# Inverting the softmax sums on GpSimd, as a power of minus one, in a cross-attention kernel

## The chip, the core and the metric

The kernel runs on one core of a Trainium2 chip. A core has five engines that work at the same time, each through its own queue in order: TensorE (PE in the profile; its weight loads are PEld), VectorE (DVE), ScalarE (ACT), GpSimd (POOL) and SyncE (SP), which here only issues DMAs. They wait for each other by semaphores. SBUF is the memory on the chip with 128 partitions; PSUM, in eight banks, takes what TensorE computes. The metric is the device time of one execution in microseconds. Before the change it is 497.91 us, the median of 2 runs (497.78 to 498.04).

## What is computed

The kernel is a cross-attention layer in float32: 2 batches of 2048 tokens with 640 channels, 20 heads of 32 channels, and a context of 154 rows a batch. The first 77 rows of the context are text, the other 77 have key and value weights of their own; each half has its own softmax, and the two results are added.

```python
text = encoder_hidden_states[:, :TEXT_LEN, :]
ip = encoder_hidden_states[:, TEXT_LEN:, :]
q = _split_heads(hidden_states @ Wq.T, H)
k = _split_heads(text @ Wk.T, H)
v = _split_heads(text @ Wv.T, H)
out_text = _merge_heads(_attend(q, k, v, sm_scale))
k_ip = _split_heads(ip @ Wk_ip.T, H)
v_ip = _split_heads(ip @ Wv_ip.T, H)
out_ip = _merge_heads(_attend(q, k_ip, v_ip, sm_scale))
out = out_text + IP_SCALE * out_ip
out = out @ Wo.T + bo
return out + residual
```

`_attend` takes softmax(q k^T / sqrt(32)) v. So each token has, for each head, two rows of 77 scores; each row has its own maximum, its own sum of exponentials, and its own inverse of that sum.

## The kernel before

The work is cut into pairs and units. A *pair* q (0 to 9) is a batch and a chunk of 128 channels, which is four heads. A *unit* u (0 to 19) is a pair and a half of the tokens, 1024 of them; unit u belongs to pair u // 2. A unit's 1024 tokens are eight tiles of 128, in three *groups* s of 3, 3 and 2 tiles (`GROUPS`). A group has its tokens on the 128 partitions and, in its free dimension, 3 x 4 x 2 x 77 = 1848 scores (12 x 154), or 1232 for the group of two tiles. So there are 20 x 3 = 60 groups, 40 large and 20 small. A large group has 24 sums for each partition, a small one 16.

A group goes through these steps, each a word in a long schedule (letter, group number, unit):

- `R`: TensorE computes the scores into four PSUM banks (`scores`, L233).
- `K`: ScalarE copies them to the buffer `pb` in SBUF (`take`, L245). For a few groups (`DIRECT`) this step is missing and the later ones read PSUM.
- `M`: VectorE finds the maxima (`maxima`, L281 and L284).
- `S`: GpSimd subtracts them (`subtract`, L295). Groups listed in `BIASED` or `DIRECT` have the subtraction in the exponential instead.
- `E`: ScalarE takes exponentials (L301 for a whole group, L269 row by row). For the 13 groups in `SUMMED` the row-by-row form also accumulates the sums, `den`.
- `D`: for the 47 other groups VectorE sums the exponentials (`sums`, L306).
- `I`: the sums are inverted, `rden` from `den` (`invert`, L311), on VectorE.
- `N`: GpSimd multiplies the group by `rden` (`normalise`, L316).
- `T`: VectorE transposes the group in blocks of 32 (`transpose`, L323).

When all six groups of a pair are transposed, `A` has TensorE multiply them with the values (`attend`, L332), and `CA` has ScalarE copy the result out (L355, L359). Between these, TensorE also computes the queries (`q`, L201), the keys and values (`k`, `v`, L142), and, from about 220 us on, the output product of the first batch (`m`, `o`, L471, L490, L500), whose parts VectorE adds up (`cm`, L515 and L521) and for which GpSimd forms differences of tokens (`G`, L431) and of weights (`W`, L401). After the last attention the output product of the second batch follows (L828 and L834 for the sums on VectorE and GpSimd, L848 for the matmuls, L792 and L794 for adding up).

The order is not found while the program runs. `SCHEDULE` is one list of such words, written out by hand; `emit` goes through it and puts each step's instructions into the queue of its engine. Each engine works strictly in that order and waits at an instruction whose inputs are not there. A piece of the list, lines 570 and 571, around three inversions:

```python
"N1.2 E0.3 M1.3 E2.3 k.2.0@4 D0.3 S1.3 q.5.0@5 LK.12 SQ.1 T1.2 VS.1.1 cq.4.1 ck.2.0 E1.3 D2.3 I0.3 R2.4@0 "
"D1.3 cq.5.0 N0.3 R0.4@1 K2.4 LK.13 v.2.0@0 VS.1.0 I2.3 K0.4 M2.4 N2.3 T0.3 E2.4 q.6.0@2 I1.3 T2.3 N1.3 "
```

The tiles `mx`, `den` and `rden` of one size rotate through four buffers each (`small`). The transposed groups lie in three zones of `pb`; a unit's zone is written again by a later unit's `K`. Loads and stores (`LK`, `LQ`, `LX`, `VS`, `SF`, `SS`) are issued by SyncE.

Of the kernel before, what the change touches and what calls it, by code (L numbers as in the profile page):

```python
# [9 lines left out]
F32 = mybir.dt.float32  # L10
AF = mybir.ActivationFunctionType
ALU = mybir.AluOpType
# [8 lines left out]
def kernel(  # L21
# [25 lines left out]
    nc = tc.nc  # L47
    P = 128
# [31 lines left out]
    const = ctx.enter_context(tc.tile_pool(name="const", bufs=1))  # L80
# [17 lines left out]
    pb = const.tile([P, SUB + 1, NT, G, LP], F32, name="pb")  # L98
    nc.gpsimd.memset(pb[:, :, :, :, 2 * L :].rearrange("p z n g l -> p (z n g) l"), 0.0)

    vT = const.tile([P, B, LP], F32, name="vT")
    nc.gpsimd.memset(vT[:, :, 2 * L :], 0.0)
    vS0 = [const.tile([P, LP], F32, name=f"vS0_{n}") for n in range(2)]
# [150 lines left out]
    dens = {}  # L254
# [53 lines left out]
    def invert(u, s):  # L308
        n = GROUPS[s][1] * G
        rden = small.tile([P, n, 2], F32, tag=f"rden{n}", name=f"rden_{u}_{s}")  # L310
        nc.vector.reciprocal(rden, dens[(u, s)])  # L311
        rdens[(u, s)] = rden

    def normalise(u, s):
# [317 lines left out]
    def emit(word):  # L632
# [28 lines left out]
        elif k[0] in "KMSEDINT":  # L661
            ps = at[f"R{i}.{x}"]
            if k[0] == "K":
                take(x, i, ps)
            elif k[0] in "ME":
                direct, biased = (x, i) in DIRECT, (x, i) in BIASED
                if k[0] == "M":
                    maxima(x, i, ps if direct else None, biased)
                elif direct or biased:
                    exponential_of(  # L670
                        x, i, ps if direct else None, den_of(x, i) if (x, i) in SUMMED else None
                    )
                else:
                    exponential(x, i)
            else:
                dict(S=subtract, D=sums, I=invert, N=normalise, T=transpose)[k[0]](x, i)
# [214 lines left out]
```

## Time and profile before

All times in microseconds, from the one profiled execution, whose span is 496.7; the median of the runs without these details is 497.91.

| what | busy | share of the span | instructions |
|---|---|---|---|
| TensorE matmuls | 490.3 | 99% | 4114 |
| VectorE | 408.5 | 82% | 412 |
| GpSimd | 362.5 | 73% | 157 |
| ScalarE | 315.0 | 63% | 1021 |

The costliest groups on VectorE and GpSimd, from the groups of the page:

| step | engine | count | busy | mean of one, ns | idle before it |
|---|---|---|---|---|---|
| normalise (L316) | GpSimd | 60 | 176.1 | 2944 | 39.7 |
| subtract (L295) | GpSimd | 38 | 119.3 | 3152 | 51.8 |
| transpose (L323) | VectorE | 60 | 115.7 | 1932 | 4.9 |
| maxima (L281) | VectorE | 51 | 93.7 | 1850 | 30.7 |
| sums (L306) | VectorE | 47 | 88.7 | 1895 | 17.6 |

Busy means that an instruction of the engine is running; an engine that waits for a semaphore is idle. PE is busy for nearly the whole span, so time before a normalisation or a transpose costs something only where PE in turn waits for it.

### The profile page before, as it was taken

What the parts mean: (1) busy time and instruction counts of PE and PEld (TensorE: products, weight loads), DVE (VectorE), ACT (ScalarE), POOL (GpSimd) and SP (SyncE); (2) the same over time, 40 slices, a digit from 0 to 9 for tenths busy, and PEclk for the clock granted to TensorE, in tenths of its full rate; (3) what the DMA queues carried; (4) which work ended last, traced back from release to release, by engine and by line L of the source; (5) the groups of instructions that cost most, each with busy time, mean ns of one, the idle gap of its engine ahead of it and who ended that gap; (6) DMA issues with size and microseconds to landing.
All of it is one profiled execution on the core that took longest, in us unless ns stands there. A gap on an engine that the chain in (4) does not pass through costs nothing.

```text
span 496.7 us, 10482 instructions
## 1 busy us (share of the span) xinstructions
PE 490.3 (99%) x4114; PEld 287.9 (58%) x4114; DVE 408.5 (82%) x412; ACT 315.0 (63%) x1021; POOL 362.5 (73%) x157
## 2 busy tenths in 40 slices
PE   8999999999999999999999999999999999999997
PEld 5676657657547556456647654755755675444442
DVE  0069989979979989969976896687999978898877
ACT  1165878978978778668999786587578966100000
POOL 0069978798888999989874858565899888284830
PEclk9999999999999999999999999999999999999999
DMA  8991440332360454886445177418525401420115
GB/s 259 356 246 40 132 120 1 106 93 69 92 213 3 132 178 132 274 273 237 158 152 191 58 244 210 133 57 246 174 69 171 127 23 43 149 84 1 43 73 223
DMA packets 67474, 69.38 MB, mean 140 GB/s; under 512 B 5473, under 2 KB 47201, under 8 KB 67425
## 3 DMA queue, kind: packets, MB, share of 16 engines
q1 hardware_dynamic: 66704, 68.00, 43.8%
q8 instruction: 32, 0.52, 0.5%
q10 hardware_dynamic: 720, 0.72, 0.4%
q14 instruction: 18, 0.14, 0.1%
HBM read 54.94 MB, written 10.49 MB: 132 GB/s over the span
## 4 chain that ended last, share of the span: by engine, by line
PE 92%; DMA 3%; SPq 1%; DVE 1%; POOL 1%; ACT 1%; issue 0%; POOLq 0%
PE bank L201 33%; PE bank L848 11%; PE bank L490 10%; PE bank L233 10%; PE bank L332 10%; PE bank L142 9%; PE bank L471 6%; PE bank L500 3%; DMA aT<-in_L_xattn_Wk_ip_dram 2%; DMA wq<-in_L_xattn_Wq_dram 2%; SPq L534 1%; POOL pb L316 1%; DVE den L306 0%; ACT pb L301 0%; SPq L132 0%
## 5 line engine op out<-in xcount | busy, mean ns | idle before, releaser
L316 POOL TENSOR_TENSOR pb<-pb,rden 128x1848 f32<-128x1848 f32 (+1 forms) x60 | 176.1, 2944 | 39.7 <-DVE rden L311 35.5
L201 PE MATMUL bank<-x,wq 128*128 128x512 f32 x400 | 180.4, 601 | 0.6 <-DMA x<-in_x_dram 0.5
L295 POOL TENSOR_TENSOR pb<-pb,mx 128x1848 f32<-128x1848 f32 (+1 forms) x38 | 119.3, 3152 | 51.8 <-DVE mx L281 51.5
L201 PEld LDWEIGHTS bank<-x,wq 128*128 128x128 f32 x400 | 74.1, 191 | 86.7 <-issue 80.8
L323 DVE STREAM_TRANSPOSE pb<-pb 128x1920 f32<-128x1920 f32 (+1 forms) x60 | 115.7, 1932 | 4.9 <-POOL pb L316 4.3
L281 DVE TENSOR_REDUCE mx<-pb 128x24 f32<-128x1848 f32 (+1 forms) x51 | 93.7, 1850 | 30.7 <-ACT pb L245 30.5
L245 ACT COPY pb<-bank 128x462 f32<-128x462 f32 (+1 forms) x204 | 87.2, 539 | 36.0 <-PE bank L233 35.4
L306 DVE TENSOR_REDUCE den<-pb 128x24 f32<-128x1848 f32 (+1 forms) x47 | 88.7, 1895 | 17.6 <-ACT pb L301 13.3
L301 ACT ACTIVATE pb<-pb 128x1848 f32<-128x1848 f32 (+1 forms) x38 | 64.2, 1696 | 17.8 <-POOL pb L295 17.5
L269 ACT ACTIVATE pb<-pb,mx 128x77 f32<-128x77 f32 x224 | 67.8, 364 | 0.3 <-DVE mx L281 0.2
L233 PEld LDWEIGHTS bank<-kT,qT 32*128 32x128 f32 x1280 | 45.4, 184 | 26.9 <-issue 15.6
L269 ACT ACTIVATE pb<-bank,mx 128x77 f32<-128x77 f32 x184 | 51.8, 386 | 9.3 <-DVE mx L284 9.3
L233 PE MATMUL bank<-kT,qT 32*128 32x154 f32 x1280 | 56.2, 305 | 0.3 <-ACT kT L559 0.3
L332 PE MATMUL bank<-pb,v 32*32 32x512 f32 x1600 | 55.2, 597 | 0.0
L142 PE MATMUL bank<-wo_ct,aT 128*128 128x154 f32 x320 | 45.6, 296 | 0.3 <-DMA aT<-in_L_xattn_Wk_ip_dram 0.3
L142 PEld LDWEIGHTS bank<-wo_ct,aT 128*128 128x128 f32 x320 | 42.9, 188 | 3.6 <-issue 2.2
L332 PEld LDWEIGHTS bank<-pb,v 32*32 32x32 f32 x1600 | 29.9, 103 | 22.8 <-issue 10.7
L211 ACT ACTIVATE qT<-bank 128x512 f32<-128x512 f32 x40 | 24.2, 619 | 22.1 <-PE bank L201 22.0
L471 PE MATMUL bank<-aT,wo_ct 128*128 128x512 f32 x80 | 36.1, 596 | 0.0
L269 ACT ACTIVATION_READ_ACCUMULATOR pb<-bank,mx 128x1 f32 x128 | 33.6, 267 | 0.0
L490 PE MATMUL bank<-aT,wo_ct 128*128 128x256 f32 x128 | 32.3, 385 | 0.0
L490 PEld LDWEIGHTS bank<-aT,wo_ct 128*128 128x128 f32 x128 | 23.7, 190 | 6.5 <-issue 3.0
(75 smaller groups left out, 434.4 us busy)
## 6 DMA issues: line engine op xcount, KB each, us to landing
x<-in_x_dram SPq DMA_DIRECT2D x20, 1280.0 KB, 6.7
out_dram<-acc SPq DMA_DIRECT2D x20, 256.0 KB, 2.3
x<-in_x_dram SPq DMA_DIRECT2D x18, 256.0 KB, 5.9
acc<-in_x_dram SPq DMA_DIRECT2D x16, 256.0 KB, 4.7
out_dram<-x SPq DMA_DIRECT2D x15, 256.0 KB, 2.0
v<-vS SPq DMA_DIRECT2D x160, 20.0 KB, 2.8
wq<-in_L_xattn_Wq_dram SPq DMA_DIRECT2D x9, 320.0 KB, 5.0
aT<-in_L_xattn_Wk_dram SPq DMA_DIRECT2D x5, 512.0 KB, 5.5
```

The lines of the kernel that those rows point to most:

```text
L142: nc.tensor.matmul(keys_in(out), loaded[n][:, k, :], cT[:, k, :, t, :], start=(k == 0), stop=(k == NCC - 1))
L201: nc.tensor.matmul(pq, wqs[q % 3][:, k, :], xs[place_of(u, h)][:, k, :], start=(k == 0), stop=(k == NC - 1),)
L233: nc.tensor.matmul(ps[g][:, ts(t, 2 * L)], qTs[(u, h)][g * D : (g + 1) * D, ts(st, P)], kT[g * D : (g + 1) * D, c, b].rearrange("p t l -> ...
L245: nc.scalar.copy(keys_of(u, s)[:, :, g], ps[g][:, : n * 2 * L].rearrange("p (n l) -> p n l", n=n))
L269: nc.scalar.activation(row, row if ps is None else rows_in(ps[g], n)[:, t, x], AF.Exp, bias=maxs[(u, s)][:, *one], accum_out=None if den i ...
L281: nc.vector.tensor_reduce(mx, rows_of(u, s), AX.X, ALU.max, negate=negate)
L295: nc.gpsimd.tensor_tensor(rows_of(u, s), rows_of(u, s), maxs[(u, s)].unsqueeze(3).to_broadcast([P, n, 2, L]), ALU.subtract)
L306: nc.vector.tensor_reduce(den_of(u, s), rows_of(u, s), AX.X, ALU.add)
L316: nc.gpsimd.tensor_tensor(rows_of(u, s), rows_of(u, s), rdens[(u, s)].unsqueeze(3).to_broadcast([P, n, 2, L]), ALU.mult)
L323: nc.vector.transpose(p, p)
L332: nc.tensor.matmul(pa[r][g * D : (g + 1) * D, :], v4s[q % 2][rows, g, k, :], zones[rows, :, g, k, :], start=(k == 0), stop=(k == NK - 1),)
L490: nc.tensor.matmul(part, w_of[m][:, kp, op], t_of(m, b, i)[:, kp], start=(op == kp == 0 and m in (1, 2, 5)), stop=(op == 1 and kp == 1 and ...
```

## The change

The reciprocal of each group's sums on VectorE becomes a two-input operation on GpSimd: the sums to the power of a constant minus one, which stands in a column of its own and is read with a step of zero for all 24 (or 16) sums. The constant is written once by a memset on GpSimd ahead of the loops. The words of the schedule keep their places, so the power enters GpSimd's queue where `I` stands: after the last `S`, `N`, `G` or `W` before it in the list and ahead of the next one, which in 48 of the 60 cases is the normalisation of the same group. The normalisation, which waited for VectorE, then follows its power on the same engine.

```diff
     pb = const.tile([P, SUB + 1, NT, G, LP], F32, name="pb")
     nc.gpsimd.memset(pb[:, :, :, :, 2 * L :].rearrange("p z n g l -> p (z n g) l"), 0.0)
 
+    minus = const.tile([P, 1], F32, name="minus")
+    nc.gpsimd.memset(minus, -1.0)
     vT = const.tile([P, B, LP], F32, name="vT")
...
     def invert(u, s):
         n = GROUPS[s][1] * G
         rden = small.tile([P, n, 2], F32, tag=f"rden{n}", name=f"rden_{u}_{s}")
-        nc.vector.reciprocal(rden, dens[(u, s)])
+        nc.gpsimd.tensor_tensor(rden, dens[(u, s)], minus.unsqueeze(2).to_broadcast([P, n, 2]), ALU.pow)
         rdens[(u, s)] = rden
```

## The prediction

> **What bounds the kernel now.** I read the page first (busy shares, the slices, the chain), then the windows by stretch, the groups by form, the waits of GpSimd (POOL), and last the timeline where TensorE (PE) is nearest to waiting.
>
> ```profile
> span 496.7 us, 10482 instructions
> ...
> PE 490.3 (99%) x4114; PEld 287.9 (58%) x4114; DVE 408.5 (82%) x412; ACT 315.0 (63%) x1021; POOL 362.5 (73%) x157
> ...
> POOL 0069978798888999989874858565899888284830
> ...
> PE 92%; DMA 3%; SPq 1%; DVE 1%; POOL 1%; ACT 1%; issue 0%; POOLq 0%
> ```
>
> PE is busy for 99% of the span and the chain is PE's for 92%. The change takes nothing off PE, so what it can do is to make PE wait. GpSimd, which gets the new work, stands at 8 or 9 tenths over long stretches. The windows cut the part with attention into four, which I chose so that each is either tight or loose for GpSimd. The second fence has the same windows for the reciprocals alone.
>
> ```profile
> core 0: us, PE busy (x) PEld busy (x) DVE busy (x) ACT busy (x) POOL busy (x), PEclk, DMA share, GB/s
> 20.00:70.00 50.00, 49.41 (x371) 31.75 (x382) 39.78 (x29) 30.94 (x67) 38.12 (x13) 1.00 0.58 164
> 70.00:255.00 185.00, 184.83 (x1918) 112.11 (x1917) 169.85 (x135) 152.62 (x430) 160.40 (x59) 1.00 0.44 135
> 255.00:347.00 92.00, 91.76 (x820) 54.28 (x789) 69.76 (x85) 70.91 (x325) 61.94 (x25) 1.00 0.54 171
> 347.00:424.00 77.00, 76.88 (x712) 49.21 (x707) 69.53 (x74) 55.19 (x191) 68.59 (x37) 1.00 0.34 105
> ```
>
> ```profile
> 20.00:70.00 50.00, 1.51 (x6) 1.00 0.58 164
> 70.00:255.00 185.00, 8.15 (x31) 1.00 0.44 135
> 255.00:347.00 92.00, 3.01 (x11) 1.00 0.54 171
> 347.00:424.00 77.00, 3.34 (x12) 1.00 0.34 105
> ```
>
> PE is idle for 0.17 + 0.24 + 0.12 = 0.53 us from 70 to 424 us: a relief can win hardly more than that. POOL is idle for 11.9, 24.6, 30.1 and 8.4 us, with 6, 31, 11 and 12 inversions to take in. How much PE has in hand shows at the attention of the pair that starts at 211.57 us (rows of POOL, DVE and PE):
>
> ```profile
> 191.59 3.29 POOL L295 TENSOR_TENSOR pb<-pb,mx 128x1848 f32<-128x1848 f32 x1 [1.00 <-DVE mx L281]
> 194.83 2.26 POOL L316 TENSOR_TENSOR pb<-pb,rden 128x1232 f32<-128x1232 f32 x1
> 197.04 3.30 POOL L295 TENSOR_TENSOR pb<-pb,mx 128x1848 f32<-128x1848 f32 x1
> 200.28 8.75 POOL L316 TENSOR_TENSOR pb<-pb,rden 128x1232 f32<-128x1232 f32 x3
> ...
> 205.45 5.79 DVE L323 STREAM_TRANSPOSE pb<-pb 128x1280 f32<-128x1280 f32 x3
> ...
> 211.57 1.92 PE L332 MATMUL bank<-pb,v 32*32 32x512 f32 x49
> ```
>
> POOL runs from 191.59 to 209.03 us with no gap, four normalisations in it; the last transpose ends at 205.45 + 5.79 = 211.24 us, and PE takes its result 0.33 us later. POOL's queue is the second bound, a third of a microsecond behind PE.
>
> **The change part by part.** Prices come from these groups (mean ns behind the comma):
>
> ```profile
> L316 POOL TENSOR_TENSOR pb<-pb,rden 128x1848 f32<-128x1848 f32 x40 | 131.3, 3288 | 24.8 <-DVE rden L311 22.7 <-ACT aT L355 1.1 <-ACT pb L245 0.6
> ...
> L316 POOL TENSOR_TENSOR pb<-pb,rden 128x1232 f32<-128x1232 f32 x20 | 45.1, 2255 | 14.9 <-DVE rden L311 12.8 <-ACT kT L686 2.1
> ...
> L311 DVE RECIPROCAL rden<-den 128x24 f32<-128x24 f32 x40 | 11.6, 290 | 5.4 <-ACT pb L269 4.8
> ...
> L834 DVE TENSOR_TENSOR pb<-aT 128x1024 f32<-128x1024 f32 x7 | 8.3, 1221 | 1.7 <-PE bank L332 1.5 <-ACT aT L359 0.2
> ...
> L834 POOL TENSOR_TENSOR pb<-aT 128x1024 f32<-128x1024 f32 x3 | 7.1, 2381 | 2.3 <-PE bank L848 2.3
> ...
> L311 DVE RECIPROCAL rden<-den 128x16 f32<-128x16 f32 x20 | 4.8, 240 | 0.8 <-ACT pb L269 0.7
> ...
> L828 POOL TENSOR_TENSOR pb<-pb,wo_ct 128x128 f32<-128x128 f32 x9 | 4.4, 500 | 10.9 <-DVE pb L828 10.9
> ...
> L401 POOL TENSOR_TENSOR x<-x,wo_ct 128x512 f32<-128x512 f32 x1 | 1.3, 1274 | 0.1
> ```
>
> *Removed:* 60 reciprocals, 11.6 + 4.8 = 16.4 us of VectorE (DVE), and the 6.2 us for which DVE stood still before them, mostly for sums that ScalarE (ACT) accumulates. DVE is not what PE waits for, beyond the 0.53 us above: I count 0. In front of a normalisation that waited, 0.29 us goes.
>
> *Added, the constant:* one memset of a column before the loops, where POOL has no other work: 0.
>
> *Added, 60 powers on POOL.* The trace has no power. Lower end: a plain operation of that size. The two forms of the normalisation give (3288 − 2255)/(1848 − 1232) = 1.68 ns an element and 0.19 us fixed, so 0.23 us for 24 elements and 0.22 for 16; less than an ordinary operation with two inputs is excluded, as this one reads two inputs too. Upper end: as much as a whole normalisation, 3.29 and 2.26 us, the costliest thing POOL does here. Between them I take a logarithm, a product and an exponential as some twenty elementary steps, each at 1.68 ns an element (the twenty is my estimate, the step is the row's): 0.19 + 24 × 0.0336 = 0.99 us and 0.19 + 16 × 0.0336 = 0.73 us, 0.90 us in the mean of 40 and 20. The nearest row in size, the 128x128 operation at 0.50 us, holds for one step an element, so I stay above it. Behind each power its normalisation waits for it on the same engine; the dependent row above (L401) started 0.1 us after its predecessor. So a group costs POOL 1.0 us, 60 us in all.
>
> *What waits behind it.* The power takes the wait for the sums that the normalisation had, so it delays nothing new by waiting: POOL's queue behind is the normalisation, then the next subtraction. In 12 of 60 places another group's instructions lie between a power and its own normalisation, mostly another power; that moves a power ahead by one place, and I add nothing. No DMA and no other queue is touched.
>
> *What of the 60 us is hidden.* POOL's own waits tell, here for 70 to 255 us:
>
> ```profile
> POOL pb L316 <- DVE rden L311: 11.5, 10, 2.5
> POOL pb L295 <- DVE mx L281: 10.9, 8, 3.0
> ```
>
> A wait before a subtraction, for maxima, comes from PE's scores and can take up lateness. A wait before a normalisation cannot, as the power needs the same sums; there the 0.29 us of the reciprocal is gained. So this stretch covers 10.9 + 10 × 0.29 = 13.8 us of 31 × 1.0: 17.2 us show. By the same count the first stretch covers 2.1 us (its other idle time is before the first group) of 6: 3.9 show. From 255 to 347 us, 11.7 + 6 × 0.29 = 13.4 cover 11: 0 show. From 347 to 424 us, 0.8 + 1.7 (two other waits) + 8 × 0.29 = 4.8 cover 12: 7.2 show. These are the rows, in that order:
>
> ```profile
> POOL pb L295 <- DVE mx L281: 30.3, 2, 28.2
> ...
> POOL pb L316 <- DVE rden L311: 20.7, 6, 6.1
> POOL pb L295 <- DVE mx L281: 11.7, 4, 5.5
> ...
> POOL pb L316 <- DVE rden L311: 5.8, 8, 2.1
> POOL x L834 <- PE bank L500: 0.9, 1, 0.9
> POOL pb L828 <- DVE pb L828: 0.8, 1, 0.8
> POOL pb L295 <- DVE mx L281: 0.8, 2, 0.6
> ```
>
> (2.1 is 30.3 less the one wait of 28.2 before the first subtraction.) Sum: 3.9 + 17.2 + 0 + 7.2 = 28.3 us. After 424 us there is no normalisation and the rest only shifts. Span 496.7 + 28.3 = 525.0 us; the median of the two runs, 497.91, lies 1.2 above the span, so the time is 526.2 us. With c for the cost of a group, the slowdown is 49c − 20.7 (49 groups in the three stretches that show), and above c = 1.22 the loose stretch adds 11c − 13.4. Were none of it covered, it would be 60 us; were every idle moment of POOL of use, (31 − 24.6) + (12 − 8.4) = 10 us.
>
> **The rivals.**
>
> *A power is a plain operation (not slower).* 0.23 and 0.22 us, c = 0.33: every stretch covers it (10.2 of 13.8 us in the longest) and the time stays at 498 us. For it: nothing on the page says that this operation is dearer than a product. Against it: reciprocals on DVE take 290 and 240 ns, 6.2 ns an element, where DVE's sum at L834 takes 1221 ns for 1024 elements, 1.2 at most. An inversion is several steps there too. It decides below c = 0.63 (a mean power of 0.53 us), where 49c − 20.7 is under 10 us, 2% of the time.
>
> *A power is the reciprocal at POOL's pace.* The same sum (L834) takes 2381 ns on POOL and 1221 on DVE, 1.95 times. So 0.57 and 0.47 us, c = 0.63, 49 × 0.63 − 20.7 = 10.2 us: 508 us, on the edge of 2%. The Trainium skill (GPSIMD Engine Reference, section 4.1, Engine selection) has that rule: elementwise work with two inputs runs about twice as slow on GpSimd as on VectorE. By that rule the time is this rival's, and the L834 rows agree with it. Against it: DVE's reciprocal is its own instruction, while a general power has an exponent to deal with.
>
> *A power is worked out at length.* As dear as the normalisation it serves, c = 2.94 + 0.1 = 3.04: 49 × 3.04 − 20.7 + 11 × 3.04 − 13.4 = 148 us, 646 us. For it: a power in software with its special cases. Against it: 24 elements would cost what 1848 cost now.
>
> *The relief decides (faster).* DVE's 22.6 us come free and some transposes are earlier. Even with free powers PE has 0.53 us to win after 70 us and 0.59 us before: 496.8 us.
>
> **How the numbers follow.** Likeliest, c of about 0.75 to 1.8 (514 to 572 us): 0.46, forecast 526.2 us. Plain operation: 0.14. POOL's pace: 0.17, half of it within 2%. At length: 0.22. Relief: 0.01. A measurement of this kernel tells about 2% (10 us) from no change: faster 0.01; within 2%, 0.14 + 0.08 = 0.22; slower, 0.46 + 0.09 + 0.22 = 0.77. The range runs from 500 us (c = 0.47, most of the plain case left out below) to 610 us (60c − 34.1 = 112 at c = 2.4, two thirds of the lengthy case left out above); about 0.2 is outside.
>
> **What would show it.** In the profile after: 60 powers on POOL by their line, each 0.7 to 1.0 us; the reciprocal's rows gone and DVE's busy time down by 16; normalisations about 0.1 us behind their powers; PE's idle time in the four windows up by 4, 17, 0 and 7 us, in waits before attention, scores and queries, and the chain going through POOL there; from the last attention to the end, the same length as now. A power under 0.5 us makes the forecast wrong towards 498 us, one above 2 us towards 600 and more; idle time of PE between 255 and 347 us would show the cover wrong.

## The result: 692.08 us, slower by 39%

The changed kernel takes 692.08 us (median of 2 runs, 691.74 to 692.42) where the kernel before takes 497.91. The ratio is 1.3906, with a 95% interval from 1.3865 to 1.3946. The prediction had the direction and the place; its time, 526.2 us, and its range up to 610 us missed by far.

### The profile after

The page of the changed kernel, its span, busy times and the rows of the slices for PE, GpSimd and the granted clock, then the chain that ended last:

```profile
span 690.6 us, 10517 instructions
...
PE 534.7 (77%) x4114; PEld 313.5 (45%) x4114; DVE 399.4 (58%) x352; ACT 315.5 (46%) x1021; POOL 584.7 (85%) x218
...
PE   9993777878669459539983996769778768939997
...
POOL 0399989999999999999999898959699999884660
PEclk9997889789789789768996999789898977979999
...
POOL 65%; PE 16%; issue 10%; DVE 4%; DMA 2%; ACT 1%; SPq 1%; POOLq 0%; DVEq 0%
```

GpSimd is busy for 584.7 us; that alone is longer than the whole kernel was. The chain, 92% PE before, is 65% GpSimd now. The groups by form (the change moved the lines down by two, so L313 is the power, L318 the normalisation, L325 the transpose, L334 the attention):

```profile
L313 POOL TENSOR_TENSOR rden<-den,minus 128x24 f32<-128x24 f32 x40 | 166.2, 4155 | 5.2 <-DVE den L308 5.2
L318 POOL TENSOR_TENSOR pb<-pb,rden 128x1848 f32<-128x1848 f32 x40 | 131.3, 3284 | 2.7
...
L325 DVE STREAM_TRANSPOSE pb<-pb 128x1920 f32<-128x1920 f32 x40 | 87.1, 2176 | 147.0 <-POOL pb L318 147.0
...
L313 POOL TENSOR_TENSOR rden<-den,minus 128x16 f32<-128x16 f32 x20 | 57.9, 2893 | 5.6 <-DVE den L308 5.5
```

Here is the cost. A power of 24 elements takes 4,155 ns, of 16 elements 2,893 ns. From the two sizes that is (4155 − 2893) / 8 = 158 ns an element and 0.37 us fixed, against 1.68 ns an element for the product that normalises: 94 times as much for each element. The power of 24 sums takes longer than multiplying the 1848 exponentials that they belong to, which still takes 3,284 ns. VectorE's transposes wait for GpSimd: 147.0 us ahead of the 40 large ones and 48.9 ahead of the 20 small ones, where VectorE had stood idle for 4.9 us ahead of all 60.

The timeline of GpSimd shows the alternation, and how a group's cost is to be measured, from the start of a power to the start of its normalisation:

```profile
95.32 2.89 POOL L313 TENSOR_TENSOR rden<-den,minus 128x16 f32<-128x16 f32 x1
98.29 2.25 POOL L318 TENSOR_TENSOR pb<-pb,rden 128x1232 f32<-128x1232 f32 x1
100.50 4.16 POOL L313 TENSOR_TENSOR rden<-den,minus 128x24 f32<-128x24 f32 x1
104.73 3.28 POOL L318 TENSOR_TENSOR pb<-pb,rden 128x1848 f32<-128x1848 f32 x1
```

A small group costs 98.29 − 95.32 = 2.97 us, a large one 104.73 − 100.50 = 4.23 us, 3.81 in the mean of 20 and 40. The chain of waits walks from one of these instructions to the next:

```profile
100.54 4.13 POOL rden L313
104.67 0.07 issue
104.73 3.28 POOL pb L318
108.02 3.25 POOL pb L297
111.27 4.12 POOL rden L313
```

### The same stretches, before and after

The prediction cut the kernel at 70, 255, 347 and 424 us; within a microsecond of each, a pair (the first, sixth, eighth and last) starts its attention. The first rows of PE's attention there, before and then after:

```profile
69.78 1.82 PE L332 MATMUL bank<-pb,v 32*32 32x512 f32 x42
...
254.63 1.92 PE L332 MATMUL bank<-pb,v 32*32 32x512 f32 x49
...
346.21 1.33 PE L332 MATMUL bank<-pb,v 32*32 32x512 f32 x32
...
423.64 1.92 PE L332 MATMUL bank<-pb,v 32*32 32x512 f32 x49
```

```profile
90.14 1.92 PE L334 MATMUL bank<-pb,v 32*32 32x512 f32 x18 [7.44 <-issue]
...
373.95 2.02 PE L334 MATMUL bank<-pb,v 32*32 32x512 f32 x32 [13.39 <-DVE pb L325]
...
495.13 1.93 PE L334 MATMUL bank<-pb,v 32*32 32x512 f32 x12 [4.63 <-ACT pb L271]
...
615.74 2.12 PE L334 MATMUL bank<-pb,v 32*32 32x512 f32 x32 [10.52 <-DVE pb L325]
```

What stands in the brackets is new: before, PE came to each of these attentions without a gap in its work; now it stands idle for 4.6 to 13.4 us ahead of each. The prediction's count, with the measured cost of a group, 4.23 and 2.97 us, in place of the assumed one, gives for each stretch:

| stretch (before) | groups, large + small | cost on GpSimd | counted as hidden | should show | grew by |
|---|---|---|---|---|---|
| to 69.8 us | 4 + 2 | 22.9 | 2.1 | 20.8 | 90.14 − 69.78 = 20.4 |
| 69.8 to 254.6 | 20 + 11 | 117.3 | 13.8 | 103.5 | 283.81 − 184.85 = 99.0 |
| 254.6 to 346.2 | 8 + 3 | 42.8 | 13.4 | 29.4 | 121.18 − 91.58 = 29.6 |
| 346.2 to 423.6 | 8 + 4 | 45.7 | 4.8 | 40.9 | 120.61 − 77.43 = 43.2 |
| to the end | none | 0 | 0 | 0 | 74.9 − 73.1 = 1.8 |

Together 194.6 counted; the span grew by 690.6 − 496.7 = 193.9 us. The close sum is partly luck: the stretches miss by −4.5 to +2.3 us, and these errors cancel.

The 1.8 us at the end are the last attention alone. Its 160 matmuls, in one row each before and after:

```profile
423.64 5.52 PE L332 MATMUL bank<-pb,v 32*32 32x512 f32 x160
```

```profile
615.74 7.34 PE L334 MATMUL bank<-pb,v 32*32 32x512 f32 x160 [10.52 <-DVE pb L325]
```

From the end of these rows to the end of the span it is 67.5 us in both kernels. The last section comes back to why the same matmuls took longer.

### The profile page after: what moved, and what is told of

It reads as the page before. It is cut to its first block, busy times and chain, and to the rows that moved or that the text cites. A ratio compares the mean times of both kernels' runs of the same rounds, so it can differ in the third digit from the quotient of the medians.

```text
span 690.6 us, 10517 instructions
## 1 busy us (share of the span) xinstructions
PE 534.7 (77%) x4114; PEld 313.5 (45%) x4114; DVE 399.4 (58%) x352; ACT 315.5 (46%) x1021; POOL 584.7 (85%) x218
## 4 chain that ended last, share of the span: by engine, by line
POOL 65%; PE 16%; issue 10%; DVE 4%; DMA 2%; ACT 1%; SPq 1%; POOLq 0%; DVEq 0%
POOL rden L313 28%; POOL pb L318 21%; POOL pb L297 13%; PE bank L850 8%; DVE mx L283 3%; PE bank L334 2%; PE bank L203 2%; POOL aT L433 1%; DMA aT<-in_L_xattn_Wk_ip_dram 1%; PE bank L492 1%; DMA wq<-in_L_xattn_Wq_dram 1%; DVE pb L325 1%; PE bank L473 1%; PE bank L235 1%; PE bank L144 1%
## 5 line engine op out<-in xcount | busy, mean ns | idle before, releaser
L313 POOL TENSOR_TENSOR rden<-den,minus 128x24 f32<-128x24 f32 (+1 forms) x60 | 223.9, 3735 | 10.7 <-DVE den L308 10.7
L325 DVE STREAM_TRANSPOSE pb<-pb 128x1920 f32<-128x1920 f32 (+1 forms) x60 | 117.2, 1954 | 195.9 <-POOL pb L318 195.9
L203 PE MATMUL bank<-x,wq 128*128 128x512 f32 x400 | 182.4, 605 | 0.5 <-DMA x<-in_x_dram 0.4
L318 POOL TENSOR_TENSOR pb<-pb,rden 128x1848 f32<-128x1848 f32 (+1 forms) x60 | 176.3, 2940 | 3.8
L334 PE MATMUL bank<-pb,v 32*32 32x512 f32 x1600 | 73.0, 761 | 75.4 <-DVE pb L325 44.7
L235 PE MATMUL bank<-kT,qT 32*128 32x154 f32 x1280 | 66.0, 333 | 49.1 <-ACT qT L213 32.6
L235 PEld LDWEIGHTS bank<-kT,qT 32*128 32x128 f32 x1280 | 52.7, 206 | 78.1 <-ACT qT L213 37.1
L334 PEld LDWEIGHTS bank<-pb,v 32*32 32x32 f32 x1600 | 38.1, 117 | 108.5 <-issue 83.9
L144 PE MATMUL bank<-wo_ct,aT 128*128 128x154 f32 x320 | 47.1, 302 | 0.9 <-ACT aT L361 0.7
L492 PE MATMUL bank<-aT,wo_ct 128*128 128x256 f32 x128 | 34.2, 402 | 6.4 <-POOL aT L433 6.4
L492 PE MATMUL bank<-aT,x 128*128 128x256 f32 x64 | 23.5, 517 | 18.8 <-DVE acc L517 11.3
```

Source lines behind the costliest of these rows:

```text
L144: nc.tensor.matmul(keys_in(out), loaded[n][:, k, :], cT[:, k, :, t, :], start=(k == 0), stop=(k == NCC - 1))
L203: nc.tensor.matmul(pq, wqs[q % 3][:, k, :], xs[place_of(u, h)][:, k, :], start=(k == 0), stop=(k == NC - 1),)
L235: nc.tensor.matmul(ps[g][:, ts(t, 2 * L)], qTs[(u, h)][g * D : (g + 1) * D, ts(st, P)], kT[g * D : (g + 1) * D, c, b].rearrange("p t l -> ...
L313: nc.gpsimd.tensor_tensor(rden, dens[(u, s)], minus.unsqueeze(2).to_broadcast([P, n, 2]), ALU.pow)
L318: nc.gpsimd.tensor_tensor(rows_of(u, s), rows_of(u, s), rdens[(u, s)].unsqueeze(3).to_broadcast([P, n, 2, L]), ALU.mult)
L325: nc.vector.transpose(p, p)
```

## The experiments

The theory: what shows is the time that GpSimd needs for a group's inversion, less the waits that were there, stretch by stretch, and only the price of a power was wrong. The rivals: the move itself costs (the place in GpSimd's queue, the hand-over from VectorE); the power is dear because of its exponent or its number of values; the cover (the waits of GpSimd that hide new work) was counted wrongly. Diffs are against the changed kernel unless said otherwise, and the times of before beside them were measured on the same chip.

### The same move with a plain operation

```diff
-        nc.gpsimd.tensor_tensor(rden, dens[(u, s)], minus.unsqueeze(2).to_broadcast([P, n, 2]), ALU.pow)
+        nc.gpsimd.tensor_tensor(rden, dens[(u, s)], minus.unsqueeze(2).to_broadcast([P, n, 2]), ALU.mult)
```

> The sums are multiplied by minus one on GpSimd in place of being raised to it; so they are not inverted, and everything else is as after the change. Theory (only the price of a power counts): the operation takes 0.22 to 0.23 us, c = 0.33 us for a group, hidden in every stretch: 498 to 500 us. Rival (the move itself counts: the inversion standing in GpSimd's queue, the hand-over from VectorE): a good part of the 194 us stays, 550 us or more.

Measured: 499.06 us beside 497.68, ratio 1.0029 (1.0017 to 1.0041). The line of the product that stands in the power's place, by form:

```profile
L313 POOL TENSOR_TENSOR rden<-den,minus 128x24 f32<-128x24 f32 x40 | 9.1, 227 | 15.6 <-DVE den L308 13.1 <-ACT pb L271 2.1 <-ACT aT L361 0.4
```

One word of the code makes 193 of the 194 us. The product takes 227 ns; the prediction's straight line through the two normalisations had given 229. Moving the step, with a product in the power's place, costs 1.4 us, more than the 0 that the count gave for it.

### Three plain operations: the cost that the prediction assumed

```diff
-        nc.gpsimd.tensor_tensor(rden, dens[(u, s)], minus.unsqueeze(2).to_broadcast([P, n, 2]), ALU.pow)
+        for src in (dens[(u, s)], rden, rden):
+            nc.gpsimd.tensor_tensor(rden, src, minus.unsqueeze(2).to_broadcast([P, n, 2]), ALU.mult)
```

> Three such products in a row, each waiting for the one before; the sums are not inverted. This gives the cost of a group that the prediction assumed: 3 x 0.225 + 3 x 0.1 = 0.97 us. Theory (the count of what is hidden was right, and only the price of the power wrong): 49 x 0.97 - 20.7 = 27 us more, 525 us. Rival (half of the idle time of GpSimd or all of it hides it, or none): 508 us if all, 556 us if none.

Measured: 521.51 us beside 497.68, ratio 1.0487 (1.0465 to 1.0509), 23.8 us more. The timeline of GpSimd:

```profile
197.08 0.23 POOL L314 TENSOR_TENSOR rden<-den,minus 128x24 f32<-128x24 f32 x1
197.38 0.53 POOL L314 TENSOR_TENSOR rden<-rden,minus 128x24 f32<-128x24 f32 x2
197.99 3.29 POOL L319 TENSOR_TENSOR pb<-pb,rden 128x1848 f32<-128x1848 f32 x1
...
210.07 0.21 POOL L314 TENSOR_TENSOR rden<-den,minus 128x16 f32<-128x16 f32 x1
210.36 0.51 POOL L314 TENSOR_TENSOR rden<-rden,minus 128x16 f32<-128x16 f32 x2
210.95 2.25 POOL L319 TENSOR_TENSOR pb<-pb,rden 128x1232 f32<-128x1232 f32 x1
```

The three cost 0.91 us in a large group and 0.88 in a small one, 0.90 in the mean, a little under the 0.97 expected. 49 × 0.90 − 20.7 = 23.4 us, and 23.8 were measured. With all of GpSimd's idle time as cover the count is 31 × 0.90 − 24.6 and 12 × 0.90 − 8.4, together 5.7 us; with none it is 54. So at the price that the prediction assumed, its own time would have come within some 5 us.

### No inversion at all

Against the kernel before:

```diff
-        rden = small.tile([P, n, 2], F32, tag=f"rden{n}", name=f"rden_{u}_{s}")
-        nc.vector.reciprocal(rden, dens[(u, s)])
-        rdens[(u, s)] = rden
+        rdens[(u, s)] = dens[(u, s)]
```

> No inversion at all: the groups are multiplied by their sums. Theory (TensorE is the bound, and the relief of VectorE is worth at most TensorE's idle time of 1.1 us between 20 and 424 us): 496.8 to 498 us. Rival (VectorE's 16 us and its waits of 6 us hold the kernel up somewhere): 490 us or less.

Measured: 497.35 us beside 497.68, ratio 0.9997 (0.9989 to 1.0006). The step that the change moves cost nothing that could be measured where it stood, so a cheaper inversion had nothing to gain here.

### Another exponent

```diff
-    nc.gpsimd.memset(minus, -1.0)
+    nc.gpsimd.memset(minus, 1.0)
```

> The sums to the power of plus one on GpSimd, so they are not inverted; the instruction is the same but for the constant. Theory (the routine works out any power at length): 4.16 and 2.89 us again, 692 us. Rival (the price comes from the exponent minus one or from what it returns): clearly under 4 us an instruction, and a time closer to 500 us.

Measured: 693.67 us; the instruction takes 4,155 and 2,894 ns, the same as before to a nanosecond:

```profile
L313 POOL TENSOR_TENSOR rden<-den,minus 128x24 f32<-128x24 f32 x40 | 166.2, 4155 | 6.2 <-DVE den L308 6.2
```

For exponents of plus and minus one there is no short way. Other exponents were not tried.

### Fewer elements, and fewer partitions

The first edit leaves the power four of a group's sums, the second leaves it 32 of the 128 partitions (`D` is 32); VectorE inverts the rest.

```diff
-        nc.gpsimd.tensor_tensor(rden, dens[(u, s)], minus.unsqueeze(2).to_broadcast([P, n, 2]), ALU.pow)
+        few = rden.rearrange("p n t -> p (n t)"), dens[(u, s)].rearrange("p n t -> p (n t)")
+        nc.vector.reciprocal(few[0][:, 4:], few[1][:, 4:])
+        nc.gpsimd.tensor_tensor(few[0][:, :4], few[1][:, :4], minus.to_broadcast([P, 4]), ALU.pow)
```

> The power for 4 of a group's sums, the reciprocal on VectorE for the other 20 or 12. Theory (158 ns an element and 0.37 us fixed, from the two sizes): 1.0 us an instruction, c = 1.08; with the reciprocals still there the cover is 2.1, 10.9, 11.7 and 2.5 us, and 60 x 1.08 = 65 us show by 38: 535 us. Rival (the price is mostly the start of the routine): 2 us or more an instruction, 590 us or more.

```diff
-        nc.gpsimd.tensor_tensor(rden, dens[(u, s)], minus.unsqueeze(2).to_broadcast([P, n, 2]), ALU.pow)
+        nc.gpsimd.tensor_tensor(
+            rden[:D], dens[(u, s)][:D], minus[:D].unsqueeze(2).to_broadcast([D, n, 2]), ALU.pow
+        )
+        nc.vector.reciprocal(rden[D : 2 * D], dens[(u, s)][D : 2 * D])
+        nc.vector.reciprocal(rden[2 * D :], dens[(u, s)][2 * D :])
```

> The power on partitions 0 to 31 alone, two reciprocals on VectorE for the other 96. Theory (the partitions are worked on side by side, and the price goes by the elements of one partition): 4.16 and 2.89 us an instruction as with all 128, about 700 us. Rival (the price goes by the number of values): a quarter of what grows with the elements, 1.3 and 1.0 us, about 545 us.

Measured: 532.14 us beside 497.61 (ratio 1.0694, 1.0663 to 1.0725) for four elements, and 695.61 us for 32 partitions. The rows by form, first of the one and then of the other:

```profile
L315 POOL TENSOR_TENSOR rden<-den,minus 128x4 f32<-128x4 f32 x60 | 60.4, 1009 | 14.8 <-DVE den L308 14.8
```

```profile
L313 POOL TENSOR_TENSOR rden<-den,minus 32x24 f32<-32x24 f32 x40 | 165.9, 4147 | 6.0 <-DVE den L308 6.0
```

Four elements: 0.37 + 4 × 0.158 = 1.00 us by the line through the two sizes, 1,009 ns measured. So the price goes by the element along the free dimension, with 0.37 us to start; and as 32 partitions take the same 4.15 us as 128, it does not go by the number of partitions. The time went up by 34.5 us where the count gave 38.

### The power in one part of the kernel only

Three kernels use the power for a part of the groups and the reciprocal on VectorE for the others. The condition is all that differs; this is the first (called e7_loose below):

```diff
-        nc.gpsimd.tensor_tensor(rden, dens[(u, s)], minus.unsqueeze(2).to_broadcast([P, n, 2]), ALU.pow)
+        if 13 <= u <= 15 or (u, s) in ((12, 0), (12, 1)):
+            nc.gpsimd.tensor_tensor(rden, dens[(u, s)], minus.unsqueeze(2).to_broadcast([P, n, 2]), ALU.pow)
+        else:
+            nc.vector.reciprocal(rden, dens[(u, s)])
```

> Powers only for the 11 groups that were inverted between 255 and 347 us before (8 large, 3 small), reciprocals on VectorE for all others. A group costs GpSimd 4.24 or 2.97 us with the step to its normalisation, 42.8 us in all. Theory (waits for maxima and the reciprocal's 0.29 us hide 13.4 us there, as the prediction counted): 29 us more, 527 us. Rivals: all idle time of GpSimd there (30.1 us) hides it: 510 us; none does: 540 us.

For the second kernel (e10_tight) the condition is `2 <= u <= 11 or (u, s) == (12, 2)`:

> Powers only for the 31 groups that were inverted between 70 and 255 us before (20 large, 11 small), reciprocals for all others; 117.4 us of GpSimd's time. Theory (13.8 us of it are hidden, and what shows in a stretch isn't won back in the next): 104 us more, 601 us. Rival (the looser stretch behind takes lateness up): up to 18 us less, 583 us.

For the third it is `u < 2 or u > 15`:

> Powers only for the 18 groups that e7_loose and e10_tight left to VectorE: units 0, 1 and 16 to 19 (12 large, 6 small), 68.7 us of GpSimd's time. Theory (each stretch adds what it can't hide, whatever the others do; 2.1 and 4.8 us are hidden): 62 us more, 559 us, and the three partial versions add up to the whole change: 33.1 + 99.7 + 62 = 195 us beside 194. Rival (stretches share their cover or lengthen each other): the sum of the three is off by 10 us or more.

| groups with the power | time | beside | ratio, interval | more by | expected |
|---|---|---|---|---|---|
| 11, loose stretch | 530.75 | 497.61 | 1.0656 (1.0638 to 1.0674) | 33.1 | 29 |
| 31, tight stretch | 597.28 | 497.61 | 1.1996 (1.1978 to 1.2014) | 99.7 | 104 |
| 18, both ends | 564.21 | 497.59 | 1.1344 (1.1325 to 1.1363) | 66.6 | 62 |

The three add up to 199.4 us beside 194.2 for the whole change: within 3% the stretches add. The loose stretch alone shows the plainest picture. These are the windows of the kernel with 11 powers:

```profile
70.00:255.00 185.00, 184.83 (x1930) 111.93 (x1902) 170.15 (x134) 152.61 (x431) 160.50 (x58) 1.00 0.43 134
255.00:347.00 92.00, 74.95 (x636) 45.64 (x623) 48.84 (x56) 52.33 (x245) 76.25 (x28) 0.91 0.40 131
```

The columns are as in the prediction: the window, its length, then PE, PEld, DVE, ACT and POOL, the clock, and DMA. Up to 255 us PE is busy for 184.83 of 185 us, as before; where the powers start, it is idle for 17 of 92 us. GpSimd had 30.1 us of idle time there and the powers need 42.8. Were its idle time all of use, 12.7 us would show; 33.1 do.

The attentions show where these 33.1 us arise. Their rows in this kernel, of the sixth and the eighth pair:

```profile
254.23 5.52 PE L337 MATMUL bank<-pb,v 32*32 32x512 f32 x160
...
375.38 9.08 PE L337 MATMUL bank<-pb,v 32*32 32x512 f32 x160 [4.64 <-ACT pb L271]
```

The stretch itself, from the start of the first row to that of the second, grew by 121.15 − 91.58 = 29.6 us, as counted: 13.2 of the 42.8 us were hidden. The other 3.5 us come behind it, and the eighth pair's attention took just that much longer, 9.08 us against 5.52 before. Read in the same way, the other two kernels show the same; the part behind a stretch is in each case what the attention at its end took beyond 5.52 us:

| groups with the power | stretches grew by | counted | behind them |
|---|---|---|---|
| 11, loose stretch | 29.6 | 29.4 | 3.5 |
| 31, tight stretch | 97.5 | 103.5 | 2.7 |
| 18, both ends | 20.1 + 40.7 | 20.8 + 40.9 | 2.1 + 1.8 |

So the count holds within 1 us in three stretches and is 6 us too high in the tight one, and the slower attentions were not in it at all. Why the tight stretch hid 6 us more than counted was not settled.

The waits of GpSimd in the loose stretch of this kernel, from 254.2 to 375.4 us:

```profile
POOL pb L297 <- DVE mx L283: 13.0, 3, 8.4
POOL rden L314 <- ACT pb L271: 3.6, 2, 2.4
POOL rden L314 <- DVE den L308: 2.9, 1, 2.9
POOL pb L321 <- DVE rden L316: 2.5, 1, 2.5
```

Before, GpSimd waited 11.7 us for maxima and 20.7 us for inverted sums there. The waits for maxima, which the prediction took as cover, are all still there, 13.0 us. What shrank are the waits for sums, to 3.6 + 2.9 + 2.5 = 9.0 us.

## Why the prediction was wrong

**What bounds it:** right. PE was the bound with 0.53 us of idle time after 70 us, GpSimd stood a third of a microsecond behind it, and the kernel without any inversion is no faster.

**The removed reciprocals, at 0:** right, by the same kernel.

**The constant, the order, what queues behind the power:** right, taken together, within the 1.4 us that the plain operation at the same place costs. The prediction's count gave 0 for that.

**The price of a power:** this step failed. The prediction took "a logarithm, a product and an exponential as some twenty elementary steps, each at 1.68 ns an element", 0.99 and 0.73 us. It is 4.16 and 2.89 us: 158 ns an element, as much as 94 steps of the normalising product. The twenty came from no row, and no run shows by what steps GpSimd works out a power. The upper end was wrong too. "As much as a whole normalisation" sounded like a bound, but nothing in the trace made it one: no row held an operation of this kind, and the dearest row of an engine bounds nothing that the engine has not been seen to do. With that end too low, the range ended at 610 us and the rival at length at 646 us, both short of 692. (60 × 2.4 − 34.1 is 110 and not the 112 of the range, which changes nothing here.)

**What is hidden:** right in the amount, wrong in the reason. With the measured cost of 3.81 us for a mean group, the formula gives 60 × 3.81 − 34.1 = 194.5 us; 194.2 were measured. The three plain operations agree with it near the assumed price too, 23.4 counted and 23.8 measured. But the prediction said which waits would give way: those for maxima "can take up lateness", and one before a normalisation "cannot, as the power needs the same sums". These are GpSimd's waits for the two in the whole kernel, before and then after:

```profile
POOL pb L295 <- DVE mx L281: 51.5, 15, 28.2
POOL pb L316 <- DVE rden L311: 35.5, 23, 6.1
```

```profile
POOL pb L297 <- DVE mx L283: 48.5, 10, 27.8
...
POOL rden L313 <- DVE den L308: 10.7, 6, 2.9
```

The waits for maxima fell by 3.0 us, where the count let them cover some 25; those for sums fell by 24.8, where the count allowed 0.29 us for each of 24 waits, 7 us. So the reason given in this step failed too. Why its amount came out nevertheless, here and in the loose stretch, is not explained and has to count as luck. A likely reason is that the powers of other groups, which now stand ahead of a power in GpSimd's queue, fill the wait for its sums; that was not tried by itself.

**The rivals:** the plain operation, 498 us, is what a product at that place does (499.06), but not a power. The reciprocal at GpSimd's pace, 508 us, is refuted: from VectorE to GpSimd, 290 ns became 4,155, 14 times and not twice. The Trainium skill (GPSIMD Engine Reference, section 4.1, Engine selection) states the factor of two for elementwise additions, products and maxima; the trace before agrees with it for the sums at L834, 2,381 ns on GpSimd and 1,221 on VectorE, and these runs show that it doesn't carry over to a power. The rival at length was the right one in kind. The relief was worth nothing.

**What would show it:** a power "above 2 us towards 600 and more" was the sign given for this outcome, and it is what the profile shows. Idle time of PE in the loose stretch, named as a sign against the cover, came as well, but at this price the prediction's own formula expects 29.4 us there, and the stretch grew by 29.6. Two smaller signs did not come: VectorE's busy time fell by 9.1 us (408.5 to 399.4) and not by 16, and the end is 1.8 us longer.

## What to carry to other kernels

Before a step is moved to another engine, that engine's price for this very operation has to be measured; the prices of its other operations do not bound it, and here a factor of 94 for each element lay between a product and a power. Where two engines are both nearly full, compare sums first: 60 inversions cost VectorE 16.4 us and GpSimd 224 us, and GpSimd had 134 us left in the span. Of the 229 us that the powers cost GpSimd, 34 did not show. The waits that gave way were not the ones that looked free, so a count of cover is tested by the waits that are left afterwards, and not by its sum alone.

## What the runs showed of the hardware that was not expected

The power on GpSimd takes 0.37 us and 158 ns for each element of a partition (1,009 ns for 4, 2,893 for 16, 4,155 for 24). It takes the same for exponents plus and minus one, and within 8 ns the same for 32 partitions as for 128.

TensorE's granted clock fell once it had to wait. The windows of the changed kernel between the attentions named above:

```profile
20.00:90.00 70.00, 50.88 (x356) 32.63 (x355) 37.00 (x23) 32.26 (x71) 58.49 (x19) 0.88 0.43 121
90.00:374.00 284.00, 204.89 (x1910) 123.71 (x1914) 166.13 (x105) 157.38 (x459) 274.36 (x89) 0.84 0.30 92
374.00:495.00 121.00, 99.70 (x788) 58.51 (x788) 67.70 (x73) 61.91 (x278) 102.10 (x37) 0.91 0.38 118
495.00:616.00 121.00, 89.89 (x724) 57.08 (x740) 68.24 (x62) 58.59 (x205) 115.51 (x50) 0.85 0.21 65
```

The granted clock is 0.84 to 0.91 there, where it was 1.00 in every window before, and TensorE's busy time rose from 490.3 to 534.7 us for the same 4114 instructions. The Trainium skill (TensorE: Matmul & The Clock Gate, Part 1) states that the clock is halved after an idle window of some 3.4 us; the trace agrees in that the granted clock fell only where TensorE waited, and to a half. These are the windows from the last wait on; TensorE's work ahead of it ends at 605.2 us:

```profile
606.00:609.00 3.00, 0.00 (x0) 0.00 (x0) 0.35 (x1) 0.00 (x0) 3.00 (x2) 1.00 0.00 0
...
612.00:615.74 3.74, 0.00 (x0) 0.00 (x1) 1.60 (x3) 0.00 (x0) 3.74 (x5) 0.50 0.44 143
...
615.74:617.50 1.76, 1.76 (x33) 0.61 (x34) 1.76 (x7) 0.00 (x0) 0.97 (x3) 0.50 0.92 204
617.50:619.00 1.50, 1.50 (x48) 0.78 (x32) 1.50 (x2) 0.00 (x0) 0.00 (x0) 0.50 1.01 393
...
621.00:623.10 2.10, 2.10 (x64) 1.07 (x45) 0.00 (x0) 0.32 (x2) 0.70 (x2) 1.00 0.03 8
```

The clock is 1.00 up to 609 us, 0.50 from 612 us on, still 0.50 for the first 3 us of the attention, and 1.00 again at its end. This attention took 7.34 us where it took 5.52 at a clock of 1.00; PE waits for nothing within it that the profile shows, and what follows it is as long as before. So by this trace the lower clock costs 1.8 us at the end of the kernel, though no run held the clock fixed. Behind the stretches of the partial kernels the clock is low in the same way, 0.63 to 0.74 in the mean of the slower attentions. For the 9.08 us of e7_loose that is not enough (5.52 / 0.70 = 7.9 us), and what else delayed it was not settled. What the lower clock costs in the stretches that GpSimd bounds was not separated: the count of GpSimd's time knows no clock, and its small error is partly luck, as said above.
